# A fused gated-attention and feed-forward layer on one core: x's differences moved in VectorE's order, and high products ahead of low ones in blocks 13 and 14

## The chip, the cores and the metric

The kernel runs on one core of a Trainium2 chip. The core has five engines that run side by side, each working through its own queue in order: PE (TensorE, matrix products; its weight loads are listed apart as PEld), DVE (VectorE), ACT (ScalarE), POOL (GpSimd) and SP (SyncE, which here only issues DMA transfers). An engine waits for another by semaphores. Products land in PSUM, which has 8 banks; everything else lies in SBUF.

The metric is the device time of one execution in microseconds (us); the median of three runs of the kernel before is 490.25 us.

## The reference, cut to what matters

Input x has 4 x 2048 tokens of 256 numbers, which are 8192 tokens in all.

```
# attention half, in chunks of 32 tokens
Q, K, V = x @ W_q.T, x @ W_k.T, x @ W_v.T
S = (Q @ K.T within a chunk) * mask           # mask[i, j] = decay**(i - j), 0 above the diagonal
h = layernorm(x + sigmoid(x @ W_g.T) * (S @ V) @ W_o.T + x)
# feed-forward half: integer weights (-127 to 127), scaled by 1/127
u = silu(h @ w_gate.T) * (h @ w_up.T)         # 768 features
out = layernorm(h + u @ w_down.T)
```

Everything is float32.

## The kernel before, in words

**Blocks and stages.** The 8192 tokens are worked on in 16 blocks of 512, numbered 0 to 15. The loop `for b in range(NB - 2)` (line 1107, NB is 16) is software-pipelined: its pass b does the feed-forward half of block b, the output side of the attention of block n = b + 2, and the input side of the attention of block m = b + 3. While m is below 16 (passes 0 to 12, `more`), a pass has all of this. Pass 13 and the code behind the loop (lines 1220 to 1391) finish blocks 13, 14 and 15.

**Products in parts.** TensorE's fast forms carry fewer bits than float32, so a factor is split. For x: `token_parts` (line 462) makes x_hi on ACT and x_lo on POOL (line 471), and returns a function, `x_gaps`, that makes x_gap, "x's differences", on DVE when it is called (line 477). One such call is two instructions `scalar_tensor_tensor` of 128x512 numbers, x_gap = x - (1 + 1/4096) * x_hi, with both inputs in SBUF. A product of x and a weight then has three kinds: 0 (high parts), 1 (low parts) and 2 (differences). `three` (line 524) issues kinds 0 and 1 for both of its banks, lets ACT multiply each bank by 1 + 1/4096 (line 531), and returns a function that issues kind 2 and then copies the banks out. For y (`split_y`) this copy is `yT` on DVE (line 556). h and u are split in two, hi on ACT (lines 859 and 908) and lo on POOL (lines 860 and 909).

**Order.** `in_turn` and `in_steady_turn` keep an instruction in program order on its engine; nearly all that this document speaks of is kept so. What one pass b from 1 to 12 issues, in this order:

- `normalize` of h of block b + 1 on ACT, then the feed-forward's hidden chunk 0 (`up_now`): products fg and fu on PE, s = silu(fg) on ACT (line 892), u = fu * s on DVE (line 903, "the first u"), u_hi on ACT, u_lo on POOL.
- Chunk 1's products and s, with its u held back (`held=True`).
- `move_h` (line 827): four 32x32-blocked transposes of h on DVE ("the squares of h", line 835) and, on SP's queue, 16 DMAs (line 842) that put the squares together to hT, which `split_h` reads late in the pass.
- Kinds 0 and 1 of y of block m on PE and the scaling on ACT; then chunk 1's held `multiply` ("the second u"), with its u_hi and u_lo.
- Chunk 2; then `y_rest`, that is kind 2 of y, which reads x_gap, and the two copies to yT on DVE.
- Chunk 3, and `attn_scores` (line 636): the products ps (line 652), which need all of yT; the masks; `attn_values`; chunk 4; the differences of the attention's output, go_gap, on DVE; v, the gate, chunk 5; the output projection p_o; `split_h`; the sums h and their moments.
- x_hi and x_lo of block m + 1, the square roots on ACT, and `ffn_down` (line 926). There `project_back` (line 718) issues the down projection fdn into two banks, all high products first, then bank 0's low ones, then bank 1's; then it calls `between` (line 1189), which computes scale and shift of h on DVE and calls `x_gaps` for block m + 1; then for each bank DVE makes the residual r (line 937) and its moments.

So x_gap of block m + 1 is made at the end of pass b, ahead of the residuals on DVE, and first read in pass b + 1 by kind 2 of y. `between` does so in passes 0 to 11. Pass 0 also calls `x_gaps` once near its start for block 3; this call is not touched.

**Blocks 13 and 14.** Here `ffn_down` is called with `chunkwise=True` (lines 949 to 969). `early_and_late` (line 920) divides the six hidden chunks: early are the high and low terms of chunks 0 to 3, late those of chunks 4 and 5. For early, and then for late, the loop goes over the two banks, and in each over the terms (high ones first) and two column halves. After a bank's late terms comes its residual on DVE. For block 13 the last terms of the attention run between early and late (`amid`). Behind block 14, POOL computes scale and shift of the output in a chain of small operations (`iterated_scale_and_shift`, line 392), and then makes the u_lo of block 15, which block 15's down projection (line 1319) reads.

Of the kernel before, what the change touches and what calls it, by code (L numbers as in the profile page):

```python
# [54 lines left out]
P = 128  # L55
# [21 lines left out]
def kernel(  # L77
# [15 lines left out]
    nc = tc.nc  # L93
    NT, D = x.shape
# [19 lines left out]
    def in_turn(ins):  # L114
        tc.keep_in_program_order(ins)
# [261 lines left out]
    def scale_and_shift(mv, std, kind, name, eng=nc.gpsimd, order=free):  # L377

        on_r, on_dst = kind
        scale, minus, shift = (  # L380
            small.tile([P, NG], F32, tag=tag, name=f"{tag}_{name}")
            for tag in ("scale", "minus", "shift")
        )
        in_turn(nc.vector.reciprocal(std, std))  # L384
        for t, sign in ((minus, -1.0), (scale, 1.0)):
            order(eng.tensor_scalar(t, std, sign * on_dst / on_r, None, ALU.mult))  # L386
        order(eng.tensor_tensor(shift, mv[:, :, 0], minus, ALU.mult))
        return scale, shift
# [438 lines left out]
    def move_h(b, h):  # L827

        sq = moved.tile([P, D // SQ, NG, SQ], F32, tag="sq", name=f"sq_{b}")
        for g in range(NG):
            in_turn(
                nc.vector.transpose(
                    sq[:, :, g, :], h[:, g, :].rearrange("p (j f) -> p j f", f=SQ)
                )
            )
        hT = moved.tile([P, KD, NQ, NG * SQ], F32, tag="hT", name=f"hT_{b}")
        for q in range(NQ):  # L840
            for j in range(NQ):
                nc.sync.dma_start(  # L842
                    hT[j * SQ : (j + 1) * SQ, :, q, :],
                    sq[q * SQ : (q + 1) * SQ, j::NQ, :, :].rearrange(
                        "p k g t -> p k (g t)"
                    ),
                )
        return hT
# [77 lines left out]
    def ffn_down(b, uT, h, between=None, chunkwise=False, amid=None):  # L926


        r = work.tile([P, NG, D], F32, tag="r2", name=f"r2_{b}")
        mv = no_moments(f"f{b}")  # L930
        made = None
        order = in_turn

        def residual(gs, pb):

            order(
                nc.vector.scalar_tensor_tensor(
                    flat(r, gs), pb, SCALE**2 / U_UP * H_UP, flat(h, gs), ALU.mult, ALU.add
                )
            )  # L940
            moments(r, f"f{b}", range(gs.start, gs.stop), order, mv)

        def begin():
            nonlocal made
            if between is not None:
                made = between()

        ws = [chunked(w) for w in fd]
        if chunkwise:
            per = TB // D  # L950
            banks = [bank(f"fdn_{b}_{k}") for k in range(NG // per)]
            for late, terms in enumerate(early_and_late(uT, ws)):
                if late and amid is not None:
                    made = amid()
                for k, pb in enumerate(banks):
                    for i, (part, w) in enumerate(terms):
                        for j in range(per):
                            g = k * per + j
                            product = nc.tensor.matmul(  # L959
                                pb[:, j * D : (j + 1) * D],  # L960
                                lhsT=part[:, g * P : (g + 1) * P],
                                rhs=w,
                                start=late + i + j == 0,
                                stop=True,
                                skip_group_check=True,
                            )
                            in_turn(product)
                    if late:
                        residual(slice(k * per, (k + 1) * per), pb)
        else:  # L970
            project_back(b, uT, ws, residual, "fdn", begin)
        return r, mv, made
# [134 lines left out]
    for b in range(NB - 2):  # L1107
        n = b + 2
        m = b + 3
        more = m < NB  # L1110
        xns[n] = load_xn(n)
        if b and m + 1 < NB:
            xTs[m + 1] = load_xT(m + 1)
        hT = hTs.pop(b)
        uT = ([], []) if b else uT_0
        sT, v, sg = ahead
        if not more:
            scales_next = iterated_scale_and_shift(mv_out, of_out, f"out_{b}")
        if b:
            normalize(hs[b + 1], *scales_h)  # L1120
            up_now(b, hT, uT, 0)
        multiply = ffn_up(b, hT, uT, range(1, 2), held=True)
        if b:
            moving = move_h(b + 1, hs[b + 1])
        else:
            cast_fd(0, range(2, 3))
            multiply()
            x_gaps()
            sT = attn_scores(n, yT)
            xTs[m + 1] = load_xT(m + 1)  # L1130
        if more:
            yT, y_rest = split_y(m, x_parts)
        if b:
            multiply()
        if not more:
            goT = attn_values(n, sT, v, sg)
        multiply = ffn_up(b, hT, uT, range(2, 3), held=True)
        if b > 1:
            normalize(r_before, *scales_out, range(NG // 2))
        multiply()  # L1140
        if more:
            y_rest()
        if b == 0:
            normalize(hs[b + 1], *scales_h)
            moving = move_h(b + 1, hs[b + 1])
        if not more:
            go_parts, go_gaps = token_parts(goT, f"go_{n}")
        multiply = ffn_up(b, hT, uT, range(3, 4), held=True)
        if b > 1:
            normalize(r_before, *scales_out, range(NG // 2, NG))  # L1150
        multiply()
        if b > 1:
            store(b - 2, r_before)
        if more:
            sT_next = attn_scores(m, yT)
            goT = attn_values(n, sT, v, sg)
            multiply = ffn_up(b, hT, uT, range(4, 5), held=True, low_first=True)
            go_parts, go_gaps = token_parts(goT, f"go_{n}")
            if b == 0:
                cast_fd(1, range(1))  # L1160
            multiply()
            go_gaps()
            v_next, v_rest = split_v(m, x_parts)
            sg_next, g_rest = split_gate(m, x_parts)
            v_rest()
            if b == 0:
                cast_fd(1, range(1, 2))
            up_with_cast(b, hT, uT, 5, 1, range(2, 3))
        else:
            up_now(b, hT, uT, 4)  # L1170
            go_gaps()
        r_before = r_out
        if more:
            hs[n], out_rest = split_out(n, go_parts)
            if b:
                hTs[b + 1] = split_h(b + 1, moving)
            g_rest()
            mv_h = out_rest()
            if b == 0:
                hTs[b + 1] = split_h(b + 1, moving)  # L1180
            ahead = sT_next, v_next, sg_next
            if m + 1 < NB:
                x_parts, x_gaps = token_parts(xTs[m + 1], f"x_{m + 1}")
            std_h = root_in_turn(mv_h, of_h, f"h_{b}")
            if b:
                mv_before, std_before = mv_out, root_in_turn(mv_out, of_out, f"out_{b}")
            back_to_silu()

            def between():
                scales = scale_and_shift(  # L1190
                    mv_h, std_h, of_h, f"h_{b}", nc.vector, in_turn
                )
                if m + 1 < NB:
                    x_gaps()
                return scales

            r_out, mv_out, scales_h = ffn_down(b, uT, hs.pop(b), between)
            if b:
                scales_out = scale_and_shift(mv_before, std_before, of_out, f"out_{b}")
        else:  # L1200
            multiply = ffn_up(b, hT, uT, range(5, KH), held=True)
            hs[n], out_rest = split_out(n, go_parts)
            multiply()
            hTs[b + 1] = split_h(b + 1, moving)
            scales_out = scales_next
            normalize(r_before, *scales_out)
            store(b - 1, r_before)

            def amid():
                return iterated_scale_and_shift(out_rest(), (HALF, 1.0), f"h_{n}")  # L1210

            r_out, mv_out, scales_h = ffn_down(
                b, uT, hs.pop(b), chunkwise=True, amid=amid
            )
            scales_out = iterated_scale_and_shift(mv_out, of_out, f"out_{b + 1}")
# [361 lines left out]
```

## Time and profile before

| what | value |
|---|---|
| median of 3 runs | 490.25 us (490.17 to 490.75) |
| the profiled execution's own time | 491.6 us |
| its span, in which all the profile's times count | 490.0 us |
| PE busy | 482.2 us, 98% of the span |
| DVE, ACT, POOL busy | 345.8, 370.8, 281.0 us |
| granted TensorE clock, mean | 0.998 |
| x_gap (line 477), 30 instructions | 677 ns shortest, 685 median, 1779 longest |
| go_gap (line 477), 30 instructions | 684 ns shortest, 1750 median, 1787 longest |

The profile lists, for one execution, every instruction with its engine, its line in the kernel and its start in us from the span's start. In a timeline's line, the first number is the start, the second the time from the first start to the last end of the merged group, then engine, line, operation, output<-inputs, shapes and count; a bracket gives the idle time of the engine before it and what ended it. In a list of waits, the numbers are total us, times and the longest. An instruction's listed end overlaps its successor's start by some 0.08 us where an engine runs without a pause. PE's times are modelled, so short waits hide in a busy PE.

### The profile page before, as it was taken

Reading aid. Unit: us, or ns where it says so; the run is one execution under the profiler, and the core shown is the slowest. Engines: PE = TensorE matmul, PEld = TensorE weight load, DVE = VectorE, ACT = ScalarE, POOL = GpSimd, SP = SyncE. Lnnn points to the kernel's source line nnn. Section 1 sums busy time; section 2 is a strip of 40 time slices with the busy share of each in tenths; the row PEclk is TensorE's granted clock in tenths of the full one; section 3 lists DMA queues with packets and bytes.
Section 4 is the critical chain, followed back from the end, with each engine's and each line's share of the span. In section 5 each row is a group of like instructions: output and inputs, shape, how many; then the busy total and the mean of one; then the engine's idle time right before and its main releaser. Section 6 shows DMA issues by size and latency. Waiting matters only on the chain.

```text
span 490.0 us, 12289 instructions
## 1 busy us (share of the span) xinstructions
PE 482.2 (98%) x4760; PEld 381.8 (78%) x4760; DVE 345.8 (71%) x795; ACT 370.8 (76%) x699; POOL 281.0 (57%) x285
## 2 busy tenths in 40 slices
PE   9999999999999999999999999999999999999995
PEld 5788786787978879687787968879687787868675
DVE  4587958758586785859767686785858767577656
ACT  4778687686876888777786877788777786776845
POOL 3835754654745567365654745566464655657764
PEclk9999999999999999999999999999999999999999
DMA  8730421121313114031141314114031211103102
GB/s 259 223 95 29 115 59 43 46 89 25 108 48 103 64 36 140 20 111 43 46 130 26 112 49 118 46 39 135 21 111 46 81 48 30 61 17 109 37 15 85
DMA packets 43323, 36.99 MB, mean 75 GB/s; under 512 B 4864, under 2 KB 39168, under 8 KB 43264
## 3 DMA queue, kind: packets, MB, share of 16 engines
q1 hardware_dynamic: 42144, 35.28, 24.5%
q10 hardware_dynamic: 1120, 0.92, 0.6%
q8 instruction: 38, 0.62, 0.6%
q14 instruction: 21, 0.17, 0.1%
HBM read 20.45 MB, written 8.39 MB: 59 GB/s over the span
## 4 chain that ended last, share of the span: by engine, by line
PE 88%; DVE 4%; ACT 4%; SPq 2%; DMA 1%; issue 1%; DVEq 0%; ACTq 0%
PE fg L883 16%; PE fu L883 15%; PE fdn L727 12%; PE p_v L512 8%; PE p_o L512 8%; PE p_g L490 8%; PE p_y L490 7%; PE po L688 3%; PE fdn L959 2%; PE ps L652 2%; SPq L842 2%; PE fdn L1319 1%; PE pg L576 1%; DVE u L903 1%; DMA wg<-in_w_gT_dram 1%
## 5 line engine op out<-in xcount | busy, mean ns | idle before, releaser
L909 POOL TENSOR_TENSOR u_lo<-u,u_hi 128x512 f16<-128x512 f32 (+1 forms) x98 | 129.4, 1325 | 83.6 <-ACT u_hi L908 80.4
L903 DVE SCALAR_TENSOR_TENSOR u<-fu,s 128x512 f32<-128x512 f32 (+1 forms) x98 | 66.1, 674 | 70.6 <-ACT s L892 69.6
L908 ACT CAST u_hi<-u 128x512 fp32r<-128x512 f32 (+1 forms) x98 | 59.6, 608 | 50.2 <-DVE u L903 50.2
L892 ACT ACTIVATE s<-fg 128x512 f32<-128x512 f32 (+1 forms) x98 | 57.5, 586 | 40.4 <-PE fg L883 40.4
L883 PE MATMUL fg<-hT_hi,fg_hi 128*128 128x512 f32 (+1 forms) x196 | 73.6, 457 | 0.0
L883 PE MATMUL fu<-hT_hi,fu_hi 128*128 128x512 f32 (+1 forms) x196 | 60.5, 390 | 0.0
L883 PE MATMUL fg<-hT_lo,fg_lo 128*128 128x512 f16 (+1 forms) x196 | 58.2, 379 | 0.0
L883 PE MATMUL fu<-hT_lo,fu_lo 128*128 128x512 f16 (+1 forms) x196 | 57.4, 375 | 0.0
L471 POOL TENSOR_TENSOR go_lo<-goT,go_hi 128x512 fp32r<-128x512 f32 x30 | 44.5, 1506 | 18.8 <-ACT go_hi L470 18.8
L477 DVE SCALAR_TENSOR_TENSOR go_gap<-go_hi,goT 128x512 fp32r<-128x512 f32 x30 | 48.2, 1645 | 0.8 <-ACT go_hi L470 0.7
L471 POOL TENSOR_TENSOR x_lo<-xT,x_hi 128x512 fp32r<-128x512 f32 x30 | 37.7, 1279 | 15.5 <-ACT x_hi L470 15.5
L883 PEld LDWEIGHTS fg<-hT_hi,fg_hi 128*128 128x128 f32 x196 | 35.6, 190 | 10.5
L883 PEld LDWEIGHTS fu<-hT_hi,fu_hi 128*128 128x128 f32 x196 | 36.5, 188 | 8.6
L792 DVE TENSOR_TENSOR h<-p_o,x 128x512 f32<-128x512 f32 x30 | 19.3, 684 | 32.7 <-PE p_o L512 30.5
L860 POOL TENSOR_TENSOR hT_lo<-hT,hT_hi 128x512 f16<-128x512 f32 x28 | 35.7, 1299 | 4.5 <-ACT hT_hi L859 4.3
L727 PE MATMUL fdn<-fd_hi,u_hi 128*128 128x256 f32 x312 | 37.6, 276 | 0.0
L727 PEld LDWEIGHTS fdn<-fd_hi,u_hi 128*128 128x128 f32 x312 | 36.5, 188 | 0.0
L883 PEld LDWEIGHTS <-fu_lo 128*128 128x128 f16 x196 | 19.2, 98 | 22.2
L727 PE MATMUL fdn<-fd_lo,u_lo 128*128 128x256 f16 x312 | 36.3, 273 | 0.0
L386 POOL TENSOR_SCALAR minus_out<-rstd_out 128x4 f32<-128x4 f32 x12 | 2.7, 221 | 56.8 <-DVE rstd_out L384 56.8
L727 PEld LDWEIGHTS <-u_lo 128*128 128x128 f16 x312 | 29.5, 98 | 3.7
L883 PEld LDWEIGHTS <-fg_lo 128*128 128x128 f16 x196 | 13.1, 98 | 19.2 <-issue 12.9
(175 smaller groups left out, 1072.6 us busy)
## 6 DMA issues: line engine op xcount, KB each, us to landing
x<-in_x_dram SPq DMA_DIRECT2D x16, 512.0 KB, 3.8
xT<-in_xT_dram SPq DMA_DIRECT2D x15, 512.0 KB, 4.6
hT<-sq SPq DMA_DIRECT2D x224, 32.0 KB, 1.9
out_dram<-r SPq DMA_DIRECT2D x13, 512.0 KB, 3.4
out_dram<-r SPq DMA_DIRECT2D x7, 128.0 KB, 1.7
fg_int<-in_ffn_gT_dram SPq DMA_DIRECT2D x3, 256.0 KB, 8.0
fu_int<-in_ffn_uT_dram SPq DMA_DIRECT2D x3, 256.0 KB, 7.1
fd_int<-in_ffn_dT_dram SPq DMA_DIRECT2D x3, 256.0 KB, 5.9
```

What stands on the lines that cost most here:

```text
L471: in_turn(nc.gpsimd.tensor_tensor(lo[:, k, :], t[:, k, :], whole, ALU.subtract))
L477: nc.vector.scalar_tensor_tensor(gap[:, k, :], whole, -WHOLE, t[:, k, :], ALU.mult, ALU.add)
L490: nc.tensor.matmul(pb, lhsT=a[kind][:, k, i * P : (i + 1) * P], rhs=b[kind][:, k, :], start=kind + k == 0, stop=True, skip_group_check=True,)
L512: nc.tensor.matmul(pb[:, j * D : (j + 1) * D], lhsT=b[kind][:, k, g * P : (g + 1) * P], rhs=a[kind][:, k, :], start=kind + k + j == 0, sto ...
L727: nc.tensor.matmul(banks[g // per][:, g % per * D : (g % per + 1) * D], lhsT=part[:, g * P : (g + 1) * P], rhs=w, start=first and g % per ...
L792: in_steady_turn(nc.vector.tensor_tensor(flat(r, gs), pb, flat(xn, gs), ALU.add))
L860: nc.gpsimd.tensor_tensor(in_order[1], whole, in_order[0].bitcast(F32), ALU.subtract)
L883: product = nc.tensor.matmul(pb, lhsT=w[kind][:, dc, hc * P : (hc + 1) * P], rhs=hT[kind][:, dc, cols], start=(kind == kinds[0] and dc == ...
L892: in_turn(nc.scalar.activation(s, pg, AF.Silu, scale=SCALE / H_UP))
L903: nc.vector.scalar_tensor_tensor(u, pu, U_UP / H_UP, s, ALU.mult, ALU.mult)
L908: in_steady_turn(nc.scalar.copy(hi, u))
L909: in_steady_turn(nc.gpsimd.tensor_tensor(lo, u, hi.bitcast(F32), ALU.subtract))
```

## The change

Two things change. First, `between` no longer calls `x_gaps`; in passes 1 to 12 it is called behind `move_h`, so DVE makes x_gap of block m behind the squares of h and in front of the second u of the same pass that reads it. Second, in the chunkwise down projection of blocks 13 and 14, early and late alike, the high terms of bank 0 and bank 1 are issued first, and then the low terms of bank 0 and bank 1; a bank's residual still follows its last low term.

```
                 if late and amid is not None:
                     made = amid()
-                for k, pb in enumerate(banks):
-                    for i, (part, w) in enumerate(terms):
-                        for j in range(per):
-                            g = k * per + j
-                            product = nc.tensor.matmul(
-                                pb[:, j * D : (j + 1) * D],
-                                lhsT=part[:, g * P : (g + 1) * P],
-                                rhs=w,
-                                start=late + i + j == 0,
-                                stop=True,
-                                skip_group_check=True,
-                            )
-                            in_turn(product)
-                    if late:
-                        residual(slice(k * per, (k + 1) * per), pb)
+                n = len(terms) // 2
+                for kind, of_kind in enumerate((terms[:n], terms[n:])):
+                    for k, pb in enumerate(banks):
+                        for i, (part, w) in enumerate(of_kind):
+                            for j in range(per):
+                                g = k * per + j
+                                product = nc.tensor.matmul(
+                                    pb[:, j * D : (j + 1) * D],
+                                    lhsT=part[:, g * P : (g + 1) * P],
+                                    rhs=w,
+                                    start=late + kind + i + j == 0,
+                                    stop=True,
+                                    skip_group_check=True,
+                                )
+                                in_turn(product)
+                        if late and kind:
+                            residual(slice(k * per, (k + 1) * per), pb)
...
         if b:
             moving = move_h(b + 1, hs[b + 1])
+            if more:
+                x_gaps()
...
             def between():
-                scales = scale_and_shift(
-                    mv_h, std_h, of_h, f"h_{b}", nc.vector, in_turn
-                )
-                if m + 1 < NB:
-                    x_gaps()
-                return scales
+                return scale_and_shift(mv_h, std_h, of_h, f"h_{b}", nc.vector, in_turn)
```

## The prediction

> **What bounds the kernel now.** I read the page first: how busy PE is, and the chain that ended last.
>
> ```profile
> PE 482.2 (98%) x4760; PEld 381.8 (78%) x4760; DVE 345.8 (71%) x795; ACT 370.8 (76%) x699; POOL 281.0 (57%) x285
> PE 88%; DVE 4%; ACT 4%; SPq 2%; DMA 1%; issue 1%; DVEq 0%; ACTq 0%
> ```
>
> PE is the bound: passes 3 to 12 take 29.2 to 29.4 us each, all busy. What another engine saves gains nothing unless PE waits for it; what it delays costs only where PE comes to wait. The list of waits of PE's weight loads shows the one place of each pass where PE already waits:
>
> ```profile
> PEld ps L652 <- DVE yT L556: 5.0, 14, 0.4
> ```
>
> I then took DVE's, POOL's, ACT's and PE's timelines of pass 9 (its first u at 317.68).
>
> ```profile
> 311.99 0.72 DVE L386 TENSOR_SCALAR minus_h<-rstd_h 128x4 f32<-128x4 f32 x1
> ...
> 312.82 1.29 DVE L477 SCALAR_TENSOR_TENSOR x_gap<-x_hi,xT 128x512 fp32r<-128x512 f32 x2
> 314.03 0.68 DVE L937 SCALAR_TENSOR_TENSOR r<-fdn,h 128x512 f32<-128x512 f32 x1
> ...
> 317.68 0.66 DVE L903 SCALAR_TENSOR_TENSOR u<-fu,s 128x512 f32<-128x512 f32 x1
> 318.25 1.41 DVE L835 STREAM_TRANSPOSE sq<-h 128x256 f32<-128x256 f32 x4
> 319.60 0.67 DVE L903 SCALAR_TENSOR_TENSOR u<-fu,s 128x512 f32<-128x512 f32 x1
> 321.58 0.69 DVE L903 SCALAR_TENSOR_TENSOR u<-fu,s 128x512 f32<-128x512 f32 x1 [1.31 <-ACT s L892]
> 322.18 1.28 DVE L556 COPY yT<-p_y 128x512 f32<-128x512 f32 x2
> ```
>
> ```profile
> 310.17 2.51 POOL L471 TENSOR_TENSOR x_lo<-xT,x_hi 128x512 fp32r<-128x512 f32 x2
> ...
> 319.07 1.29 POOL L909 TENSOR_TENSOR u_lo<-u,u_hi 128x512 f16<-128x512 f32 x1 [0.65 <-ACT u_hi L908]
> ```
>
> ```profile
> 318.37 0.62 ACT L908 CAST u_hi<-u 128x512 fp32r<-128x512 f32 x1 [2.48 <-DVE u L903]
> ...
> 319.39 1.07 ACT L531 ACTIVATE p_y<-p_y 128x512 f32<-128x512 f32 x2
> 320.37 0.61 ACT L908 CAST u_hi<-u 128x512 fp32r<-128x512 f32 x1
> 320.88 0.60 ACT L892 ACTIVATE s<-fg 128x512 f32<-128x512 f32 x1
> ```
>
> ```profile
> 320.52 0.82 PE L490 MATMUL p_y<-x_gap,m_gap 128*128 128x512 f32 x2
> ...
> 323.54 0.76 PE L652 MATMUL ps<-yT,xT 128*32 128x32 f32 x64
> ```
>
> The reader is to see a chain without slack: second u (319.60), its u_hi (320.37), the third s (320.88), the third u (321.58), two yT (322.18 to 323.46), and ps 0.08 later. ps comes 0.56 us behind the last pair of fu products (322.98), where pairs of this kind follow each other by 0.47: PE waits about 0.09. Any delay of the second u therefore reaches PE, less 0.07: its u_hi could start 0.70 behind it (as the first one's does, 0.69) but starts 0.77 behind it, since ACT ends p_y just then.
>
> **Part 1, removed from `between`.** Two x_gap take 314.03 - 312.82 = 1.21 us of DVE. Without them the first residual starts at 312.82; its bank is ready: without x_gaps in its `between`, pass 12 has fdn at 425.21 and r at 429.46, 4.25 later, here 308.06 + 4.25 = 312.31. Residuals, moments, reciprocal and the first u are then 1.21 earlier, the first u at 316.47 (its s ends at 315.90). PE gains nothing: fg and fu of chunk 0 do not wait. The squares start at 317.04 and their 16 DMAs on SP, some 11 us, are 1.2 earlier too; hT is read some 16 us later, and the store and the load of xT queued behind them come earlier. POOL's scale and shift of the output move ahead of u_lo alike.
>
> **Part 1, added behind the squares.** Squares end 1.92 behind the first u (319.60 - 317.68), at 318.39. Were the gaps as short as before, the second u would stand where it stood, at 319.60. But u_lo of the first u now starts at 316.47 + 1.39 = 317.86 and holds POOL to 319.14, so the first gap meets it. What a DVE operation with its inputs in SBUF does beside a POOL operation is shown in three places: minus_h above, 0.72 instead of the 0.17 that it takes beside an idle POOL in pass 12, ends at 312.71 as x_lo does at 312.68; go_gap beside go_lo has a median of 1750 ns against x_gap's 685; and near the start:
>
> ```profile
> 18.77 2.66 DVE L477 SCALAR_TENSOR_TENSOR x_gap<-x_hi,xT 128x512 fp32r<-128x512 f32 x2
> 21.35 0.67 DVE L293 TENSOR_REDUCE top<-fg_int 128x1 f32<-128x512 int32 x1
> ```
>
> ```profile
> 19.12 1.75 POOL L447 TENSOR_TENSOR wo_lo<-wo,wo_hi 128x512 fp32r<-128x512 f32 x1
> ```
>
> The second of these gaps ends 0.56 behind wo_lo's end (20.87), and the next instruction starts 0.48 behind it: it waited for POOL's instruction to end. The squares, and u with one input in PSUM, show no such thing: the last two squares and the second u run beside the first u_lo now, at their usual 0.40 and 0.67.
>
> So the first gap is over at 319.14 + 0.48 = 319.62; the second has no POOL operation to meet (the second u_lo comes behind the second u) and takes 0.605: the second u at 320.23, 0.63 late. Its u_hi at 320.93 (+0.56), and everything behind it on ACT and DVE with it: third s 321.44, third u 322.14, yT done at 324.02, ps at 324.10. **0.56 us per pass.** Queued behind the gaps on DVE are both u and both yT; ACT holds back s, the normalized r and two u_hi behind the second u_hi; the fourth s would be 0.2 late, which ps, later by more, covers. Kind 2 of y, at 320.52, finds its second gap done at 320.31: a cover of 0.2 us, and if it went, PE would wait there instead and not twice, since ps comes later. In pass 1 the same steps from its first u (83.18) put the second u at 85.74 instead of 85.12, and ps 0.55 later. Times 12 passes: 6.6 us, all of it PE waiting.
>
> The Trainium skill, "SBUF — State Buffer", section "Who interferes with whom", says the same as a lock: a VectorE instruction with two SBUF inputs and a GpSimd instruction that reads SBUF exclude each other for a whole instruction. Against it stands the plain reading of go_gap's row, a gap 1.06 us longer whenever POOL is busy: two of them would make 2.1 less 0.07 per pass, 25 us; by the lock only the first pays, and only to u_lo's end, 6.6 us. minus_h and the gap near the start end with POOL's instruction, so this trace agrees with the lock.
>
> **Part 2.** Block 13's early and late parts take 3.54 and 1.75 us. A pair of changes from high to low and back costs 0.03 to 0.04 there (16 products: 1.03 + 0.80, against 0.91 + 0.88 for eight of each unbroken); two pairs fewer in each block save 0.07 per block, 0.14 in all. PE waits for no u_hi or u_lo there, so nothing else is gained. Against that, bank 0's last low term comes behind four more products: 0.41 later. In block 13 DVE is late anyway (r at 452.41, the bank done by 450). In block 14 DVE waits for that bank:
>
> ```profile
> 469.21 0.69 DVE L937 SCALAR_TENSOR_TENSOR r<-fdn,h 128x512 f32<-128x512 f32 x1 [2.78 <-PE fdn L959]
> ```
>
> ```profile
> 475.57 6.73 POOL L909 TENSOR_TENSOR u_lo<-u,u_hi 128x512 f16<-128x512 f32 x7
> ```
>
> Residuals, moments and POOL's chain move by 0.41, and with them block 15's seven u_lo, which run without a pause. Chunk 3's ends at 479.48 and would end at 479.89; its first product is due at about 479.79 (479.46 and three products), its weight load 0.1 before, and PE comes 0.07 sooner: PE waits 0.2 to 0.3. With the savings part 2 comes to +0.15, between -0.14 (no wait) and +0.4 (all of the shift).
>
> **Sum.** 6.6 + 0.15 = 6.75 us: span 490.0 to 496.75. The profiled execution took 491.6, which is 1.35 over the median; the difference goes onto the median: 490.25 + 6.75 = 497.0 us.
>
> **Rivals.**
>
> 1. The gaps are not held up behind the squares. For it: the second u, beside the same u_lo now, isn't. Then the second u stays at 319.60, its u_hi no longer waits for p_y, which ACT does 0.3 earlier, and each pass gains 0.07 to 0.09: -0.8 to -1.1, with part 2 about 489.5 us. It decides if u_lo is over before the squares are (0.75 sooner than reckoned), or starts behind the gaps. Against it: first u, u_lo and squares keep their distances, whatever moves. No change by measurement, or just faster.
> 2. Both gaps are held up, if POOL's small operations for the output's scale (free in their order) fall between, or something else of POOL. The pair then costs 2.58, as the pair at 18.77, instead of 1.21: 1.37 - 0.07 = 1.3 per pass, 15.6 in all, 506 us. Against it: nothing of POOL is ready between the first u_lo and the second.
> 3. The hold is there, but PE gets most of it back: 0.2 per pass, 2.4 in all, 492.7 us. Against it: no pass has idle PE time behind ps in which to catch up.
>
> **How the numbers follow.** The forecast has 0.80, rivals 1, 2 and 3 have 0.10, 0.06 and 0.04. The forecast's own bounds: from below rival 3's 0.2 per pass; from above a first gap as long as go_gap's median, 1.75, and so a second u 1.07 late, 1.0 per pass: 12.0 + 0.4 = 12.4, 502.7. The range 492.7 to 502.7 leaves out rivals 1 and 2. A measurement tells 0.2% (0.98 us) from no change: rival 1 splits into 0.07 within that and 0.03 faster; I add 0.01 to "same" for an early rival 3. Slower has 0.89.
>
> **What would show it.** Right: x_gap behind the squares with a first instruction of about 1.3 us that ends with u_lo, a second of 0.69; first u 1.2 earlier against fdn; "ps <- yT" for 0.5 us and more in 12 passes, passes of 29.85 us; p_y of kind 2 not waiting. Wrong: x_gap at 0.69 both, or passes of 29.3. In the tail, r of block 14 0.4 later against the end of fdn, and line 1319's low products waiting for u_lo. What I may have missed is an order in which u_lo does not meet the gaps.

## The result, and the profile after

The changed kernel takes 497.51 us (median of 4 runs, 496.65 to 497.67) against 490.5 us before (now the median of 4 runs): a ratio of 1.0137 with a 95% interval of 1.0119 to 1.0155, that is 7.0 us more, between 5.8 and 7.6. The forecast was 497.0 us. The profiled execution took 497.43 us, its span is 495.9.

The page after, first its busy times, then the chain that ended last:

```profile
PE 484.8 (98%) x4760; PEld 382.9 (77%) x4760; DVE 355.1 (72%) x795; ACT 372.3 (75%) x699; POOL 280.8 (57%) x285
PE 65%; DVE 12%; ACT 3%; issue 2%; DVEq 0%; ACTq 0%
```

The busy shares tell next to nothing: PE is at 98% in both. The chain tells it: PE's share falls from 88% to 65%, DVE's rises from 4% to 12%. In order of time, the chain of pass 10 after the change reads (start, us, what; the list leaves out short pieces, such as u_hi):

```profile
351.45 0.65 DVE sq L835 x2
352.11 1.84 DVE x_gap L477 x2
353.95 0.61 DVE u L903
355.11 0.60 ACT s L892
355.79 0.69 DVE u L903
356.48 1.21 DVE yT L556 x2
357.73 0.70 PE ps L652 x46
```

Before, this stretch of the chain was PE's own products. Now it leaves PE just ahead of the squares and returns at ps. The instructions of that pass on DVE (the two gaps also one by one), POOL and PE:

```profile
350.12 0.66 DVE L903 SCALAR_TENSOR_TENSOR u<-fu,s 128x512 f32<-128x512 f32 x1
350.69 1.41 DVE L835 STREAM_TRANSPOSE sq<-h 128x256 f32<-128x256 f32 x4
352.03 1.92 DVE L477 SCALAR_TENSOR_TENSOR x_gap<-x_hi,xT 128x512 fp32r<-128x512 f32 x2
353.87 0.68 DVE L903 SCALAR_TENSOR_TENSOR u<-fu,s 128x512 f32<-128x512 f32 x1
```

```profile
352.03 1.32 DVE L477 SCALAR_TENSOR_TENSOR x_gap<-x_hi,xT 128x512 fp32r<-128x512 f32 x1
353.27 0.68 DVE L477 SCALAR_TENSOR_TENSOR x_gap<-x_hi,xT 128x512 fp32r<-128x512 f32 x1
```

```profile
351.51 1.29 POOL L909 TENSOR_TENSOR u_lo<-u,u_hi 128x512 f16<-128x512 f32 x1 [0.65 <-ACT u_hi L908]
355.28 1.28 POOL L909 TENSOR_TENSOR u_lo<-u,u_hi 128x512 f16<-128x512 f32 x1 [2.48 <-ACT u_hi L908]
```

```profile
346.98 0.71 PE L883 MATMUL fg<-hT_hi,fg_hi 128*128 128x512 f32 x2
...
356.62 0.63 PE L883 MATMUL fu<-hT_hi,fu_hi 128*128 128x512 f32 x2
357.18 0.27 PE L652 MATMUL ps<-yT,xT 128*32 128x32 f32 x8
357.73 0.70 PE L652 MATMUL ps<-yT,xT 128*32 128x32 f32 x56 [0.28 <-DVE yT L556]
358.35 1.16 PE L688 MATMUL po<-sT,v 64*64 64x64 f32 x64
```

The same pass on PE before the change:

```profile
342.63 0.71 PE L883 MATMUL fg<-hT_hi,fg_hi 128*128 128x512 f32 x2
...
352.82 0.76 PE L652 MATMUL ps<-yT,xT 128*32 128x32 f32 x64
353.52 1.16 PE L688 MATMUL po<-sT,v 64*64 64x64 f32 x64
```

From the start of the pair to the next instruction, the two gaps take 353.87 - 352.03 = 1.84 us instead of 1.21. The first gap takes 1.32 us, the second its usual 0.68, and u_lo its usual 1.29: the first gap alone pays. The first u_lo ends at 352.80; 0.48 from there to the start of the instruction behind the first gap and 0.605 for the second gap make 353.88, and the second u starts at 353.87.

Counted from the pass's first fg product (346.98), yT is done at 10.69 (356.39 + 1.28), instead of 10.12 before (351.47 + 1.28, fg at 342.63): 0.57 later. Before, all of ps stood at 10.19; now 8 of its records stand at 10.20 and the other 56 at 10.75. What follows ps, the products po, starts at 11.37 instead of 10.89 (353.52 - 342.63): 0.48 later.

The waits of PE's weight loads, total, times and longest:

```profile
PEld ps L652 <- DVE yT L556: 10.2, 24, 0.8
...
PEld L1318 <- POOL u_lo L909: 0.3, 1, 0.3
```

This wait for yT has doubled (5.0 before), and block 15's down projection waits for u_lo, which it did not before. The list of PE's own waits, apart from its weight loads, is clearer: before the change it names yT once, after it 15 times (first line before, second line after):

```profile
PE ps L652 <- DVE yT L556: 0.3, 1, 0.3
PE ps L652 <- DVE yT L556: 4.3, 15, 0.4
```

From fdn to fdn (starts as the chain lists them, some 0.17 us behind the timeline's), the ten passes 3 to 12 take 29.80 us each (133.15 to 431.18) instead of 29.29 (132.46 to 425.38): 0.51 us a pass on the average. The usual pass takes 29.77, which is 0.48 more.

**Where the 5.9 us between the two spans lie.** The start of pass 0's hT_hi, which waits for transfers, differs from execution to execution: 72.76 us in the profile before, 72.22 in the one after. From there to the fdn of pass 12 it is 352.62 before and 358.96 after: the 12 passes cost 6.34 us, 0.53 each. From that fdn to the end it is 64.62 and 64.72: blocks 13 to 15 cost 0.10.

### The profile page after: what moved, and what is told of

It is laid out like the page before. It is cut to its first block, busy times and chain, and to the rows that moved or that the text cites. A ratio compares the mean times of both kernels' runs of the same rounds, so it can differ in the third digit from the quotient of the medians.

```text
span 495.9 us, 12311 instructions
## 1 busy us (share of the span) xinstructions
PE 484.8 (98%) x4760; PEld 382.9 (77%) x4760; DVE 355.1 (72%) x795; ACT 372.3 (75%) x699; POOL 280.8 (57%) x285
## 4 chain that ended last, share of the span: by engine, by line
PE 65%; DVE 12%; ACT 3%; issue 2%; DVEq 0%; ACTq 0%
PE fdn L727 12%; PE fg L883 12%; PE fu L883 11%; PE p_v L512 7%; PE p_o L512 7%; PE p_g L490 7%; DVE x_gap L477 4%; DVE u L903 3%; PE po L688 3%; DVE yT L556 2%; PE fdn L961 2%; ACT s L892 2%; PE ps L652 2%; PE p_y L490 1%; DVE sq L835 1%
## 5 line engine op out<-in xcount | busy, mean ns | idle before, releaser
L792 DVE TENSOR_TENSOR h<-p_o,x 128x512 f32<-128x512 f32 x30 | 19.3, 685 | 32.6 <-PE p_o L512 30.4
L477 DVE SCALAR_TENSOR_TENSOR x_gap<-x_hi,xT 128x512 fp32r<-128x512 f32 x30 | 28.4, 986 | 0.0
```

Of the source, the lines that this page charges most:

```text
L477: nc.vector.scalar_tensor_tensor(gap[:, k, :], whole, -WHOLE, t[:, k, :], ALU.mult, ALU.add)
L792: in_steady_turn(nc.vector.tensor_tensor(flat(r, gs), pb, flat(xn, gs), ALU.add))
```

## The experiments

**Part 1 alone.** The kernel before with x's differences behind the squares:

```
             moving = move_h(b + 1, hs[b + 1])
+            if more:
+                x_gaps()
...
             def between():
...
-                if m + 1 < NB:
-                    x_gaps()
```

> Part 1 alone: x_gap behind the squares in passes 1 to 12, the down projections of blocks 13 and 14 as before. Theory (all of the price is the first gap's wait for the first u_lo of POOL): 0.47 us per pass, 5.7 to 6.9 us over the kernel before, and passes of 29.75 us. Rival (the order of high and low products in blocks 13 and 14 has a good part of it): under 5 us over the kernel before.

Measured: 497.49 us against 490.43, ratio 1.0135 (1.0119 to 1.015), which is 5.8 to 7.4 us. The wait is that of the full change:

```profile
PEld ps L652 <- DVE yT L556: 10.3, 24, 0.8
```

From fdn to fdn passes 3 to 12 take 29.82 us each. Within this interval part 1 is the whole loss.

**Part 2 alone.** The chunkwise loop of the changed kernel, with `between` as before.

> Part 2 alone: high products of both banks ahead of low ones in blocks 13 and 14, x_gap where it was. Theory: the products' own time falls by 0.13 us, and block 15 then waits about 0.3 us for u_lo: +0.1 us in all, no difference that can be measured (-0.2 to +0.4). Rival: over 1 us slower.

Measured: 490.54 us against 490.43, ratio 0.9999 (0.9990 to 1.0008). No difference that can be measured. Its trace shows the wait that was expected, at the low products of block 15:

```profile
PEld L1321 <- POOL u_lo L909: 0.3, 1, 0.3
```

**The gaps ahead of the squares.** These first two experiments say which part costs, not why. Here as much of DVE's work stands between the two u as in part 1, but the gaps come first:

```
+            if more:
+                x_gaps()
             moving = move_h(b + 1, hs[b + 1])
...
             def between():
...
-                if m + 1 < NB:
-                    x_gaps()
```

> As part 1 alone, but x_gap ahead of the squares of h instead of behind them. Just as much of DVE's work stands between the first and the second u, but both gaps are issued before the first u_lo starts. Theory (the hold by u_lo): u_lo waits for a gap instead of a gap for u_lo, the second u stands where it stood before the change, passes of 29.2 to 29.3 us, the kernel at the time of before or up to 1 us under it. Rival (the gaps' place ahead of the second u costs, whatever POOL does): 5.7 to 6.9 us over the kernel before, as part 1 alone.

Measured: 490.64 us against 490.43, ratio 1.0002 (0.9991 to 1.0013). DVE and POOL of one pass:

```profile
315.35 0.66 DVE L903 SCALAR_TENSOR_TENSOR u<-fu,s 128x512 f32<-128x512 f32 x1
315.93 1.31 DVE L477 SCALAR_TENSOR_TENSOR x_gap<-x_hi,xT 128x512 fp32r<-128x512 f32 x2
317.16 1.41 DVE L835 STREAM_TRANSPOSE sq<-h 128x256 f32<-128x256 f32 x4
318.50 0.65 DVE L903 SCALAR_TENSOR_TENSOR u<-fu,s 128x512 f32<-128x512 f32 x1
```

```profile
316.75 1.65 POOL L909 TENSOR_TENSOR u_lo<-u,u_hi 128x512 f16<-128x512 f32 x1 [0.65 <-ACT u_hi L908]
```

Now u_lo is the one that waits: 1.65 us instead of 1.29, while the gaps take their 1.23. It delays no pass. The squares run beside it at their usual pace. The gaps' place ahead of the second u costs nothing by itself; the rival falls.

**The gaps behind the second u.** There DVE waited for the third s before the change:

```
         if b:
             multiply()
+            if more:
+                x_gaps()
...
             def between():
...
-                if m + 1 < NB:
-                    x_gaps()
```

> As part 1 alone, but x_gap behind the second u, where DVE waited 1.3 us for the third s before. Theory: the second u comes 1.2 us earlier than before, the gap waits at most 0.2 us for u_lo in time that DVE has free, kind 2 of y finds the gaps 0.1 to 0.2 us ahead, yT is early, and ps no longer waits its 0.09 us in a pass: 0.5 to 1.2 us under the kernel before. Rival (with so little ahead of kind 2 of y, PE waits there for x_gap): slower than before by 0.2 us and more in a pass, 2 us and more in all.

Measured: 489.71 us against 490.43, ratio 0.9986 (0.9977 to 0.9996): 0.7 us faster than before (0.2 to 1.1), and the lowest ratio of these runs. The reason given for it was half wrong. DVE, and PE at ps:

```profile
317.49 1.34 DVE L477 SCALAR_TENSOR_TENSOR x_gap<-x_hi,xT 128x512 fp32r<-128x512 f32 x2
319.72 0.69 DVE L903 SCALAR_TENSOR_TENSOR u<-fu,s 128x512 f32<-128x512 f32 x1 [0.90 <-ACT s L892]
320.33 1.28 DVE L556 COPY yT<-p_y 128x512 f32<-128x512 f32 x2
```

```profile
319.02 1.28 PE L490 MATMUL p_y<-x_gap,m_gap 128*128 128x512 f32 x4
...
321.48 0.63 PE L883 MATMUL fu<-hT_hi,fu_hi 128*128 128x512 f32 x2
322.04 0.76 PE L652 MATMUL ps<-yT,xT 128*32 128x32 f32 x64
```

yT is done at 321.61, 0.43 us ahead of ps, and still ps comes 0.56 behind the last fu pair, as it did before. The list of waits of PE's weight loads goes on naming yT there:

```profile
PEld ps L652 <- DVE yT L556: 4.0, 11, 0.4
```

PE's own list has no wait for yT here. So there was no wait of 0.09 us in a pass to be saved, and passes 3 to 12 take 29.29 us as before. From pass 0's hT_hi (71.83) to pass 12's fdn (423.88) it is 352.05 us, 0.57 less than before; as the later passes are equal, this lies in passes 1 and 2. In pass 1, PE waited 0.9 us at kind 2 of y for the scaling of p_y before, since the first u came late; the earlier first u moves that scaling forward, and 0.3 us of this wait are left. In the steady passes the rival's wait at kind 2 of y did not come: the gaps are done at 318.83, 0.19 ahead of it.

**u_lo kept away from the gaps.** The purest test: DVE's order is that of part 1 alone, only POOL's first u_lo is held back and made to start behind a small operation that reads x_gap (`late_lows` keeps it until it is called). Against part 1 alone:

```
-            up_now(b, hT, uT, 0)
+            ffn_up(b, hT, uT, range(1), late_low=more)
...
             if more:
                 x_gaps()
+                seen = small.tile([P, NG], F32, tag="seen", name=f"seen_{b}")
+                in_turn(
+                    nc.gpsimd.tensor_scalar(
+                        seen, x_parts[2][:, KD - 1, TB - NG :].bitcast(F32), 1.0, None, ALU.mult
+                    )
+                )
+                late_lows.pop()()
```

> As part 1 alone, with DVE's order untouched: x_gap behind the squares, in front of the second u. Only POOL is changed: the first u_lo of passes 1 to 12 stands behind a small operation of POOL (128x4) that reads the end of x_gap, so it can't start before the gaps are done. Theory (the price is the gaps' meeting with this u_lo and nothing else): two gaps in 1.21 us, the second u where it stood in the kernel before, passes of 29.2 to 29.4 us, the time of before within 1 us. Rival (the gaps' place, or the late x_gap for kind 2 of y, costs by itself): at least 3 us over the kernel before.

Measured: 490.3 us against 490.67, ratio 0.9996 (0.9987 to 1.0006). DVE and POOL:

```profile
317.13 1.25 DVE L477 SCALAR_TENSOR_TENSOR x_gap<-x_hi,xT 128x512 fp32r<-128x512 f32 x2
318.30 0.69 DVE L905 SCALAR_TENSOR_TENSOR u<-fu,s 128x512 f32<-128x512 f32 x1
```

```profile
318.47 0.22 POOL L1140 TENSOR_SCALAR seen<-x_gap 128x4 f32<-128x4 f32 x1 [2.51 <-DVE x_gap L477]
318.66 2.52 POOL L914 TENSOR_TENSOR u_lo<-u,u_hi 128x512 f16<-128x512 f32 x2
```

The gaps take 1.17 us, the passes 29.29, and all of the 7 us is gone, although POOL has more to do and starts u_lo 3.45 us behind the first u (315.21) instead of 1.39. With the same order on DVE, the meeting with u_lo is shown to be the cause.

**u_lo twice.** The opposite: POOL makes the first u_lo twice in a row. Against part 1 alone:

```
-                    in_steady_turn(nc.gpsimd.tensor_tensor(lo, u, hi.bitcast(F32), ALU.subtract))
+                    for _ in range(2 if twice else 1):
+                        in_steady_turn(
+                            nc.gpsimd.tensor_tensor(lo, u, hi.bitcast(F32), ALU.subtract)
+                        )
...
-            up_now(b, hT, uT, 0)
+            ffn_up(b, hT, uT, range(1), twice=more)
```

> As part 1 alone, but POOL makes the first u_lo of passes 1 to 12 twice, one operation right behind the other, with the same result. Theory (a gap waits until a POOL operation ends, and DVE has the next turn): the first gap ends 0.56 us behind the first u_lo as in part 1 alone, the second waits for the whole second u_lo: the pair takes about 1.1 us more, ps comes 1.6 us late in a pass, and the kernel takes 18 to 20 us over the kernel before. Rival (gaps beside POOL only run slower, at the 1.75 us of go_gap each): the pair 3.4 us instead of 1.84, ps 2.1 us late, 24 to 26 us over the kernel before. Rival (only the first gap is hurt, whatever POOL does): 5.7 to 7 us, as part 1 alone.

Measured: 509.97 us against 490.67, ratio 1.04 (1.0384 to 1.0416), 19.3 us above the kernel before. DVE and POOL, merged and then one by one:

```profile
329.83 2.99 DVE L477 SCALAR_TENSOR_TENSOR x_gap<-x_hi,xT 128x512 fp32r<-128x512 f32 x2
332.75 0.68 DVE L903 SCALAR_TENSOR_TENSOR u<-fu,s 128x512 f32<-128x512 f32 x1
```

```profile
329.31 2.97 POOL L911 TENSOR_TENSOR u_lo<-u,u_hi 128x512 f16<-128x512 f32 x2 [0.65 <-ACT u_hi L908]
```

```profile
329.31 1.29 POOL L911 TENSOR_TENSOR u_lo<-u,u_hi 128x512 f16<-128x512 f32 x1 [0.65 <-ACT u_hi L908]
329.83 1.31 DVE L477 SCALAR_TENSOR_TENSOR x_gap<-x_hi,xT 128x512 fp32r<-128x512 f32 x1
330.68 1.60 POOL L911 TENSOR_TENSOR u_lo<-u,u_hi 128x512 f16<-128x512 f32 x1
331.07 1.76 DVE L477 SCALAR_TENSOR_TENSOR x_gap<-x_hi,xT 128x512 fp32r<-128x512 f32 x1
```

The pair of gaps takes 332.75 - 329.83 = 2.92 us, 1.08 more than with one u_lo (1.1 expected), and the two u_lo take 2.97 instead of about 2.5. One by one, the first u_lo takes its usual 1.29 and the first gap 1.31, then the second u_lo 1.60 instead of 1.29 and the second gap 1.76 instead of 0.68: they take turns, whole instructions at a time. POOL's second u_lo ends at 332.28, and the next DVE instruction starts 0.47 behind it. A pass (fdn at 319.50 and 350.35) takes 30.85 us, 1.56 more than before. By its own list PE now waits in two places, at kind 2 of y for x_gap (5.6 us, 13 times) and at ps for yT (8.2 us, 24 times). Gaps that only ran slower beside POOL would have taken 3.4 us and the kernel 24 us or more; gaps of which only the first can be hurt would have left it at 497. Both rivals fall.

## Why the prediction was right, point by point

- **PE is the bound and DVE is relieved for nothing:** right. The first residual starts right behind shift_h, and the first u of pass 10 comes 3.14 us behind the pass's first fg (350.12 - 346.98) instead of 4.33 before (346.96 - 342.63): 1.19 earlier, 1.21 reckoned. PE gains nothing from it in the steady passes.
- **The gaps meet the first u_lo, which holds the first of them to its end:** right. The pair takes 1.84 us, as reckoned (320.23 - 318.39); part 1 with a later u_lo (1.17) and with u_lo ahead twice (2.92) shows the cause. The lock of the Trainium skill ("SBUF — State Buffer", section "Who interferes with whom") agrees with both; the plain reading of go_gap's row (25 us in the change) does not.
- **The delay goes through to ps undiminished, 0.56 us:** the path is right, "undiminished" isn't. In the steady passes yT is done 0.57 later, but what follows ps starts 0.48 later. The cover at kind 2 of y held in passes 2 to 12. In pass 1 PE waited there 0.4 us for x_gap, where it had waited 0.9 us for ACT's scaling before; counted from pass 0's hT_hi, ps's larger part came 0.57 later there (89.08 - 72.22 = 16.86, before 89.05 - 72.76 = 16.29), 0.55 reckoned.
- **0.56 us per pass of PE's time:** slightly mis-sized; the usual pass costs 0.48, passes 3 to 12 cost 0.51 on the average, and the 12 together 6.34 instead of 6.6. The step at fault is that ps needs all of yT, which left the chain no slack. The first products of ps need only the first half: 8 of the 64 records of ps stand at 357.18 in pass 10, in time in which PE otherwise waits, and po starts 0.62 behind the other 56 (358.35), where it started 0.70 behind all 64 before (353.52 and 352.82): 0.08 us a pass. In passes 1 and 2, where the first u, and with it yT, came late before the change already, the price was 0.64 and 0.59. It is in part luck that the total comes so near 6.6: 0.3 us of it is one pass with an idle time of DVE that nobody reckoned with (below). That PE waited 0.09 us before ps was wrong too, as the gaps behind the second u showed; it was no term of the sum, but it was the gain that rival 1 gave each pass, and that gain does not exist in the steady passes.
- **Part 2 about +0.15, between -0.14 and +0.4:** right. Fdn of pass 12 to block 15's first down product takes 53.65 us instead of 53.78, so the reordered products save 0.13; the wait for u_lo, 0.3 us, and what follows take back 0.23; the sum is 0.10.
- **Sum, 6.75 us:** 6.44 in the traces, counted from pass 0's hT_hi, and 7.0 in the medians, with an interval that holds both. The profiled execution of the kernel before (491.6 us) lies 1.1 us above its median, that of the changed kernel at its median; 0.54 of the 1.1 can be what the first one's hT_hi comes later. Where the rest lies isn't settled.
- **Rivals:** none of the three came. In the experiments, rival 1 is the pass of the gaps ahead of the squares and that of the held u_lo, both at the time of before; rival 2 is the doubled u_lo, 1.56 us a pass against the 1.3 reckoned for it.

## What to carry to other kernels

When an instruction moves on DVE and both its inputs are in SBUF, look at what POOL runs at its new time, and remember that the move itself shifts POOL's work: here the gaps' removal brought u_lo forward by 1.19 us, straight into them. A meeting is only as costly as what waits behind the instruction that loses the turn; the same pair of instructions was free 1.3 us earlier (ahead of the squares) and 0.6 us later (behind the second u), since there POOL lost the turn, or DVE had idle time. An engine that is 71% busy can still stand on a chain with hardly any slack (0.1 us here), and the chain, not the share, tells it.

## What the runs showed that was not expected

- DVE and POOL took turns by whole instructions where both had two in a row: two gaps and two u_lo took 2.92 and 2.97 us, from starts 0.52 us apart.
- A chain with hardly any slack passes on what used to be hidden. In the fdn-to-fdn pass that starts at 281.96 after the change, DVE stood idle for 0.22 us before the first u, with nothing in the profile that it waited for, and the pass took 30.06 us instead of 29.8; part 1 alone has the same idle time at 290.85. So have the gaps ahead of the squares (at 286.21) and behind the second u (at 286.00), but there the pass took 29.43 and 29.29 us. What it is stays open.
- A wait of PE's weight loads need not be a wait of PE: the 0.36 us listed at ps before cost nothing in a steady pass, since ps stood at the same 0.56 us behind the last fu pair when yT came 0.43 us early, with the same idle time listed. PE's own list names one wait for yT before the change, not 14.
- Moving the gaps behind the second u is 0.14% (0.04 to 0.23) faster than the kernel before. By the traces, what it gains lies in passes 1 and 2, not in the steady passes.
